# Two experts, one per token: dense passes for three of four batches replaced by blocks of 128 slots of one expert

## The chip, the cores and the metric

The kernel runs on one NeuronCore of a Trainium2 chip. The core has a matrix engine (TensorE, PE in the profile), a vector engine (VectorE, DVE), a scalar engine with function tables (ScalarE, ACT), a general engine (GpSimd, POOL) and SyncE (SP), which here only issues DMA transfers. The engines run beside each other and wait for each other by semaphores. The metric is the device time of one execution in microseconds (us); lower is better. The time before is the median of three runs, 1477.36 us (1475.82 to 1480.7).

## The reference, cut to what matters

`x` has 4 batches of 256 tokens of 256 numbers (`B`=4, `S`=256, `D`=256), all fp32. It goes through four layers, each a cross attention to 512 context rows and then a feed-forward part of a different kind, each on the layer norm of `x` and added to `x`. The change touches the feed-forward part of layer 2:

```python
scores = jax.nn.softmax(jnp.einsum('bsh,eh->bse', x, Wg), axis=-1)
top_expert = jnp.argmax(scores, axis=-1)
h0 = jax.nn.gelu(jnp.einsum('bsh,fh->bsf', x, W0a) + b0a, approximate=False)
out0 = jnp.einsum('bsf,hf->bsh', h0, W0b) + b0b
h1 = jax.nn.relu(jnp.einsum('bsh,fh->bsf', x, W1a) + b1a)
out1 = jnp.einsum('bsf,hf->bsh', h1, W1b) + b1b
mask0 = (top_expert == 0).astype(x.dtype)[..., None]
return out0 * mask0 + out1 * (1.0 - mask0)
```

Every token takes the output of one of two experts, and the experts differ in their weights and in their function (gelu or relu). Each has a hidden width of 512 (`F2`). The cross attention of layers 1 to 3 has 16 heads of 128 over 512 context rows. Layer 1's feed-forward part has eight experts, two for each token.

## The kernel before

The whole program is one long list of instructions for each engine, written out by hand: within `tc.manual_schedule` the order of TensorE, ScalarE, VectorE and GpSimd is the order of the calls in the code, and SyncE's DMAs also go in program order. A token's row lies on a partition, 128 tokens to a chunk, two chunks to a batch (`NC`=2). Where a matmul needs the features on partitions, TensorE transposes the chunk against the identity and ScalarE copies the result from PSUM.

**Attention 2** (`attention(2, ...)`) runs over 32 units, four batches by eight pairs of heads (`b`, `hp`). In each unit, TensorE makes the next unit's queries (`seven`, L1785, with VectorE putting the products together in `four`, L1794 to L1798), then four score matmuls and four context matmuls of 512 columns (`heads`, L1815 and L1821) with ScalarE's exponentials (L1818) between. GpSimd adds exponentials in halves (L1832, for the last unit L1830), VectorE sums them (`summed`, L1840 to L1846). For each quarter of a batch (four units), `quotients` takes the reciprocal of the sums (a matmul `pz`, L1853), `divided` spreads it (L1867) and multiplies the heads' outputs by it on GpSimd (L1868), `o_sums` makes sums of blocks on GpSimd (L1710 to L1713), and `Output` multiplies with the folded output weights (`pao`, `pbo`). The very last quarter goes through `last_output` (`py`, L1903), which is plain matmuls. A callback `after(b, hp)` is called at the end of each unit, so other work can be woven in: in attention 2 it is `beside2`. A second callback, `at_end`, is called before `last_output`.

`beside2` adds layer 1's last outputs (`Back`, whose indirect DMAs on GpSimd fetch rows), loads weights, and for the batches that are done computes the layer norm that layer 2's experts need: `Norm` (statistics on VectorE, a power on GpSimd L920) at hp 4, `tokens` (two VectorE operations, L925) at hp 5, `turned2` (four transposes L2484, a copy on ScalarE L2485) at hp 6. The last batch's is done after attention 2.

**Layer 2's experts** follow as a dense pass: for each batch `chosen2` computes the two logits with small matmuls of two columns (L2547) and a mask; `rise2` computes both experts' hidden layer for all 256 tokens (L2527, 16 matmuls of 256 columns; gelu with bias on ScalarE L2535, relu with bias on VectorE L2539); `fall2` computes both outputs (L2564, 16 matmuls of 256 columns for a batch), adds the bias (L2572) and adds output times mask to `x_sb` (L2574). In between stand the eight steps of `fold`, which multiply layer 3's attention weights together (`pm` L985, `pn` L1001, copies L993 and L1004) from raw weights that SyncE loads (`load_raw`). After it come `layernorm_T` of batch 0 for attention 3, and `bound` (L1666 to L1684), three small matmuls with VectorE maxima between, which check that the folded weights keep the exponentials in range.

**Layer 1's experts**, earlier in the program, use the scheme that the change brings to layer 2: tokens are ranked by expert, a list of tokens per block is made with matmuls, an indirect DMA gathers a block's rows (L2294), the expert's number is loaded into registers (`values_load`, L2308), and the block's weights are copied from the big weight tile by that register (L2313).

## Time and profile before

| what | value |
|---|---|
| median of three runs | 1477.36 us |
| the profiled execution | 1483.07 us |
| its span, first to last instruction | 1481.3 us |
| mean granted TensorE clock | 0.989 of full |
| attention 2, with scores | 713.5 to 1009.3 us |
| end of attention 2 | 1009.3 to 1043.4 us |
| layer 2's experts, with the folds | 1043.4 to 1119.8 us |
| attention 3 | 1119.8 to 1455 us |

How to read the profile: a row of a group has the line of the code, the engine, the operation, the tiles it writes and reads (the program's names, without numbers), how often it ran, and its durations. An fp32 matmul leaves two records. Matmuls are pipelined, so the length of one record is longer than the time between two. Rows of a timeline have start, duration, engine, line, operation and tiles, and in brackets how long the engine sat idle before it and what released it. Rows of a stage table have the stretch, its length, and then the busy time of TensorE, its weight loads, VectorE, ScalarE and GpSimd with the number of instructions, the granted clock, and what DMA did. "Chain" is the chain of work that ended last, followed back from the end.

### The profile page before, as it was taken

The numbers are of one execution on the slowest core, as the hardware profiler recorded it, in microseconds if no ns is written. First come the engines' busy times: TensorE is split into PE (matmuls) and PEld (weight loads), VectorE is DVE, ScalarE is ACT, GpSimd is POOL, SyncE is SP. The second block draws the span as 40 slices with busy tenths as digits, with TensorE's granted clock in tenths as the row PEclk, the third lists the DMA queues.
The fourth block names the chain that finished last, engine by engine and source line by source line (L and its number), as shares of the span: only waits on it lengthen the run. The fifth ranks groups of instructions, "written<-read, shape, count | busy, mean of one in ns | idle before, by whom it ended". The sixth has DMA issues, their size and how long they took to land.

```text
span 1481.3 us, 20094 instructions
## 1 busy us (share of the span) xinstructions
PE 1445.1 (98%) x7457; PEld 955.4 (64%) x7457; DVE 905.6 (61%) x1953; ACT 576.1 (39%) x1111; POOL 664.4 (45%) x780
## 2 busy tenths in 40 slices
PE   8999999999999999999999999999999999999997
PEld 7666567565566666877555666665886566666656
DVE  5566774566666556543666665656445666767675
ACT  4566443433433332244543333333233433333341
POOL 2122232476555454131466655656003665455560
PEclk8899999999999999999999999999999999999999
DMA  5000021210000000163110000000310100000000
GB/s 164 2 1 2 24 84 36 71 38 0 8 1 8 1 0 30 47 202 98 43 51 5 11 1 1 1 0 0 107 36 29 33 1 1 1 1 0 1 0 32
DMA packets 47270, 43.38 MB, mean 29 GB/s; under 512 B 8057, under 2 KB 43610, under 8 KB 47164
## 3 DMA queue, kind: packets, MB, share of 16 engines
q1 hardware_dynamic: 44188, 35.59, 7.9%
q0 software_dynamic: 1872, 5.11, 1.3%
q8 instruction: 61, 1.00, 0.3%
q10 hardware_dynamic: 1104, 1.31, 0.3%
q14 instruction: 45, 0.37, 0.1%
HBM read 36.89 MB, written 5.11 MB: 28 GB/s over the span
## 4 chain that ended last, share of the span: by engine, by line
PE 88%; DVE 6%; POOL 3%; issue 2%; ACT 0%; DVEq 0%; POOLq 0%
PE ps L1815 21%; PE po L1821 21%; PE paq L1785 5%; PE pao L1785 4%; PE pbq L1785 4%; PE pbo L1785 3%; PE pgu L2321 2%; PE ph L2527 2%; PE po L2564 2%; PE ps L1321 2%; PE po L1331 2%; PE pyf L1448 2%; PE paf L1398 1%; PE py L1903 1%; PE pm L985 1%
## 5 line engine op out<-in xcount | busy, mean ns | idle before, releaser
L1832 POOL TENSOR_TENSOR half<-pT 128x1024 f32<-128x1024 f32 x93 | 218.9, 2354 | 371.6 <-ACT pT L1818 327.9
L1815 PE MATMUL ps<-qT,cT 128*128 128x512 f32 x768 | 345.5, 592 | 0.0
L1821 PE MATMUL po<-pT,c_sb 128*128 128x512 f32 x768 | 345.2, 592 | 0.0
L1818 ACT ACTIVATE pT<-ps,mbias 128x512 f32<-128x512 f32 x384 | 263.9, 687 | 154.7 <-PE ps L1815 143.4
L1821 PEld LDWEIGHTS po<-pT,c_sb 128*128 128x128 f32 x768 | 145.9, 190 | 183.7 <-issue 183.7
L1815 PEld LDWEIGHTS ps<-qT,cT 128*128 128x128 f32 x768 | 138.8, 190 | 137.9 <-issue 137.2
L1825 ACT COPY oT<-po 128x512 f32<-128x512 f32 x96 | 56.3, 587 | 263.5 <-PE po L1821 263.5
L1868 POOL TENSOR_TENSOR oT<-oT,wide 128x512 f32<-128x512 f32 x90 | 116.3, 1312 | 28.8 <-DVE wide L1867 28.8
L1325 ACT ACTIVATE pT<-ps 128x512 f32<-128x512 f32 x128 | 66.1, 602 | 44.2 <-PE ps L1321 44.0
L1795 DVE TENSOR_TENSOR qT<-qT,paq 128x128 f32<-128x128 f32 x90 | 25.5, 283 | 87.5 <-ACT qT L1794 87.4
L1840 DVE TENSOR_TENSOR half<-half 128x512 f32<-128x512 f32 x96 | 72.2, 752 | 8.1 <-POOL half L1832 4.4
L1795 DVE TENSOR_TENSOR w<-w,pao 128x128 f32<-128x128 f32 x21 | 6.0, 286 | 109.2 <-ACT w L1794 109.2
L1842 DVE STREAM_TRANSPOSE turned<-half 128x512 f32<-128x512 f32 x96 | 68.3, 711 | 6.3
L1785 PEld LDWEIGHTS paq<-xnT_a,m_sb 128*128 128x128 f32 x360 | 58.0, 191 | 21.5 <-PE po L1821 10.5
L1785 PE MATMUL paq<-xnT_a,m_sb 128*128 128x128 f32 x360 | 71.1, 279 | 0.1
L1785 PE MATMUL paq<-xx,m_x 128*128 128x128 f32 x360 | 69.8, 276 | 0.0
L1846 DVE TENSOR_REDUCE sums<-turned 128x16 f32<-128x512 f32 x96 | 65.8, 686 | 3.3
L1785 PE MATMUL pao<-n_x,ox 128*128 128x128 f32 x336 | 65.2, 276 | 0.3 <-POOL ox L1711 0.3
L1867 DVE STREAM_TRANSPOSE wide<-rz 128x512 f32<-128x512 f32 x96 | 62.2, 685 | 0.1
L1794 ACT COPY qT<-paq 128x128 f32<-128x128 f32 x90 | 24.0, 266 | 87.1 <-PE paq L1785 87.1
L1798 DVE TENSOR_TENSOR qT<-qT,pbq 128x384 f32<-128x384 f32 x90 | 49.8, 554 | 9.4
L1785 PEld LDWEIGHTS paq<-xx,m_x 128*128 128x128 f32 x360 | 54.7, 192 | 0.1
(397 smaller groups left out, 2614.3 us busy)
## 6 DMA issues: line engine op xcount, KB each, us to landing
wo<-in_L_wo SPq DMA_DIRECT2D x12, 512.0 KB
wq<-in_L_wqT SPq DMA_DIRECT2D x11, 512.0 KB
yd<-yr SPq DMA_DIRECT2D x23, 128.0 KB
w<-in_F_w SPq DMA_DIRECT2D x4, 512.0 KB
wk<-in_L_wkT SPq DMA_DIRECT2D x11, 128.0 KB
wv<-in_L_wvT SPq DMA_DIRECT2D x11, 128.0 KB
x_sb<-in_x SPq DMA_DIRECT2D x4, 256.0 KB
wa<-in_F_aT SPq DMA_DIRECT2D x1, 1024.0 KB
```

What stands on the lines that cost most here:

```text
L1325: nc.scalar.activation(pT[kp][:, j], ps[j], AF.Exp)
L1785: nc.tensor.matmul(p[:, at, :], lhsT=lhsT, rhs=rhs, start=(k == 0 and at == 0), stop=(k == len(of) - 1 and i == which[-1]),)
L1815: nc.tensor.matmul(ps, lhsT=cT[:, b, k * P : (k + 1) * P], rhs=qT, start=True, stop=True)
L1818: nc.scalar.activation(pT[:, k, :], ps, AF.Exp, bias=mbias[:, b, k : k + 1])
L1821: nc.tensor.matmul(po, lhsT=c_sb[:, b, k, :], rhs=pT[:, k], start=(k == 0), stop=(k == NK - 1))
L1825: done["head"] = nc.scalar.copy(raw, po).ins
L1832: nc.gpsimd.tensor_tensor(half, pT[:, 0:2], pT[:, 2:4], ALU.add)
L1840: nc.vector.tensor_tensor(part, half[:, 0], half[:, 1], ALU.add)
L1842: nc.vector.transpose(turned.rearrange("p f i -> p (f i)"), part)
L1846: nc.vector.tensor_reduce(sums[b, hp // 4][:, hp % 4, :], turned, AX.X, ALU.add)
L1867: nc.vector.transpose(wide, rzs[b, hp // 4][:, hp % 4, :, None].to_broadcast([P, NB, 32]))
L1868: eng.tensor_tensor(outs[b, hp], outs[b, hp], wide.rearrange("p f i -> p (f i)"), ALU.mult)
```

## The change

For batches 0 to 2 (768 tokens in 6 chunks) each token is computed by its own expert only. The tokens are ranked within attention 2, those of expert 0 and those of expert 1 fill separate blocks, 7 blocks of 128 slots in all, and each block is one expert's. Batch 3, whose attention ends last, stays dense.

- In `beside2`, `Norm` and `tokens` come two units and one unit earlier. The normed rows are written to DRAM (`xd2`) by SyncE. The logits are now made by four VectorE operations per batch that multiply and sum along the row (`chosen2`), with the router's weights spread over all partitions. `turned2` is gone. In the last batch's units, `ranks2` (hp 5: three small matmuls, some two dozen VectorE operations) and `lists2` (hp 6: six small matmuls) make the lists; then blocks 0 and 1 are gathered by GpSimd's indirect DMAs and their first weights copied (hp 6), and blocks 2 and 3 gathered (hp 7).
- At the end of attention 2 and before `last_output`, `end2` transposes two blocks and computes the first block's hidden matmuls.
- In the block loop, block j+1's hidden layer is computed ahead of block j's output. The function is chosen with multipliers: ScalarE computes the gelu, GpSimd the relu times 0 or 1, VectorE puts them together (`either`). ScalarE copies the second weights by register, VectorE the first ones. The output rows go to DRAM (`yd2`), and `Back2` gathers them into the tokens' order on GpSimd, six times, and adds them to `x_sb`.
- Batch 3's dense pass follows the loop, with the eight folds after and between it instead of through the whole pass.
- `bound` is cut in pieces with `yield`, which are run in attention 3 at b=0, hp 3, 5 and 7.

```diff
--- before.py
+++ after.py
@@ -1669,10 +1669,12 @@
...
         nc.vector.tensor_reduce(bm[:1], pb[:1, :], AX.X, ALU.max)
+        yield
...
         nc.vector.tensor_reduce(bc[: B * NK], pc[: B * NK, :], AX.X, ALU.max)
+        yield
...
         nc.vector.tensor_scalar(over, bm[:1], -1.0, 1.0, ALU.mult, ALU.add)
+        yield
...
+    N6 = (B - 1) * NC
+    NBLK2 = (N6 * P + 2 * (P - 1)) // P
+    FK = F2 // P
+    FA = ND * F2 + FK
...
-    def turned2(b, xn):
...
+    def chosen2(xn, name):
+        lg = small.tile([P, NC, 2], F32, tag="lg2", name=f"lg2_{name}")
         for c in range(NC):
+            for e in range(2):
+                all_ = f2x.tile([P, D], F32, tag="all2", name=f"all2_{name}_{c}_{e}")
+                nc.vector.scalar_tensor_tensor(
+                    all_, xn[:, c, :], 1.0, wg2[:, :, e], ALU.mult, ALU.mult, accum_out=lg[:, c, e : e + 1]
+                )
+        return lg
+    def taken_by(b, xn):
+        lg = chosen2(xn, f"{b}")
...
+    def ranks2():
+        pr = bank("t", [P, N6 + 1], "prank2")
+        nc.tensor.matmul(pr[:, :N6], lhsT=utri, rhs=takes2, start=True, stop=False)
+        nc.tensor.matmul(pr[:, :N6], lhsT=ones, rhs=taken2[:, :N6], start=False, stop=True)
+        nc.tensor.matmul(pr[:, N6:], lhsT=ones, rhs=taken2[:, N6:], start=True, stop=True)
+        rk = tile2("rk", [P, N6 + 1])
+        nc.vector.tensor_copy(rk, pr)
...
+        nc.vector.tensor_tensor(slot, slot, d, ALU.add)
...
+        for n in range(N6):
+            nc.vector.tensor_scalar(ats[n // NC][:, n % NC, :], lane2, ln[:, n : n + 1], None, ALU.is_equal)
+        sel = tile2("sel", [P, 2, NBLK2])
+        nc.vector.tensor_scalar(sel[:, 1], begins2[:, :NBLK2], nb, None, ALU.is_ge)
+        nc.vector.tensor_scalar(sel[:, 0], sel[:, 1], -1.0, 1.0, ALU.mult, ALU.add)
+        ebi = tile2("ebi", [1, NBLK2], I32)
+        nc.vector.tensor_copy(ebi, sel[:1, 1])
+        where = tile2("where", [P, N6], I32)
+        nc.vector.tensor_copy(where, slot)
+        state2.update(bring=bring, ats=ats, sel=sel, ebi=ebi, where=where)
+    def lists2():
+        pl = bank("t", [P, NBLK2], "plist2")
+        for n in range(N6):
+            nc.tensor.matmul(
+                pl, lhsT=state2["ats"][n // NC][:, n % NC, :], rhs=state2["bring"][:, n, :],
+                start=(n == 0), stop=(n == N6 - 1),
+            )
+        who = state2["who"] = tile2("who", [P, NBLK2], I32)
+        nc.vector.tensor_copy(who, pl)
+    class Block2:
+        def __init__(self, j):
+            self.j = j
+        def gather(self):
+            self.xg = state2["pool"].tile([P, D], F32, tag="xg", name=f"xg2_{self.j}", bufs=4)
+            nc.gpsimd.indirect_dma_start(
+                out=self.xg, out_offset=None, in_=xd2[:, :],
+                in_offset=bass.IndirectOffsetOnAxis(ap=state2["who"][:, self.j : self.j + 1], axis=0),
+            )
+        def turn_in(self):
+            pt = bank("t", [P, ND, P], f"pxg2_{self.j}")
             for d in range(ND):
-                nc.tensor.transpose(pt[:, d, c * P : (c + 1) * P], xn[:, c, d * P : (d + 1) * P], ident)
-        nc.scalar.copy(xnT2[b], pt)
+                nc.tensor.transpose(pt[:, d, :], self.xg[:, d * P : (d + 1) * P], ident)
+            self.xgT = state2["pool"].tile([P, ND, P], F32, tag="xgT", name=f"xgT2_{self.j}", bufs=3)
+            nc.scalar.copy(self.xgT, pt)
+        def weights(self):
+            j = self.j
+            self.e = nc.values_load(
+                state2["ebi"][0:1, j : j + 1], engines=[E.DVE, E.Activation], min_val=0, max_val=1,
+                skip_runtime_bounds_check_because="the outcome of a comparison",
+            )
+            self.wa = f2x.tile([P, FA], F32, tag="wa", name=f"wa2_{j}", bufs=2)
+            nc.vector.tensor_copy(self.wa[:, None, :], w2a[:, bass.ds(self.e, 1), :])
+        def others(self, fp):
+            self.wb = fp.tile([P, FK, D], F32, tag="wb", name=f"wb2_{self.j}")
+            nc.scalar.copy(self.wb[:, None], w2b[:, bass.ds(self.e, 1)])
+        def rise(self):
+            j = self.j
+            ph = bank("s", [P, FK, P], f"pb2_{j}")
+            for k in range(FK):
+                for d in range(ND):
+                    nc.tensor.matmul(
+                        ph[:, k, :], lhsT=self.wa[:, d * F2 + k * P : d * F2 + (k + 1) * P], rhs=self.xgT[:, d, :],
+                        start=(k == 0 and d == 0), stop=(k == FK - 1 and d == ND - 1),
+                    )
+            self.z = f2x.tile([P, FK, P], F32, tag="z2", name=f"z2_{j}")
+            nc.vector.tensor_tensor(
+                self.z, ph, self.wa[:, ND * F2 :, None].to_broadcast([P, FK, P]), ALU.add
+            )
+        def gelu(self, fp):
+            j = self.j
+            self.g = fp.tile([P, FK, P], F32, tag="g2", name=f"g2_{j}")
+            nc.scalar.activation(self.g, self.z, AF.Gelu)
+            self.r = fp.tile([P, FK, P], F32, tag="r2", name=f"r2_{j}")
+            nc.gpsimd.tensor_scalar(self.r, self.z, 0.0, state2["sel"][:, 1, j : j + 1], ALU.max, ALU.mult)
+        def either(self, fp):
+            j = self.j
+            self.h = fp.tile([P, FK, P], F32, tag="hb2", name=f"hb2_{j}")
+            nc.vector.scalar_tensor_tensor(
+                self.h, self.g, state2["sel"][:, 0, j : j + 1], self.r, ALU.mult, ALU.add
+            )
+        def fall(self, fp):
+            j = self.j
+            py = bank("mm", [P, D], f"pyb2_{j}")
+            for k in range(FK):
+                nc.tensor.matmul(
+                    py, lhsT=self.h[:, k, :], rhs=self.wb[:, k, :], start=(k == 0), stop=(k == FK - 1)
+                )
+            y = fp.tile([P, D], F32, tag="yb2", name=f"yb2_{j}", bufs=3)
+            done["slots2"] = nc.vector.tensor_tensor(y[:, None, :], py[:, None, :], b2b[:, bass.ds(self.e, 1), :], ALU.add).ins
+            nc.sync.dma_start(yd2[j * P : (j + 1) * P, :], y)
+    class Back2:
+        def __init__(self, n):
+            self.b, self.c = divmod(n, NC)
+            self.y = state2["pool"].tile([P, D], F32, tag="xg", name=f"yg2_{n}", bufs=4)
+            nc.gpsimd.indirect_dma_start(
+                out=self.y, out_offset=None, in_=yd2[:, :],
+                in_offset=bass.IndirectOffsetOnAxis(ap=state2["where"][:, n : n + 1], axis=0),
+            )
+        def add(self):
+            xc = x_sb[self.b][:, self.c, :]
+            nc.vector.tensor_tensor(xc, xc, self.y, ALU.add)
+    blocks2 = [Block2(j) for j in range(NBLK2)]
 
     def beside2(b, hp):
@@ -2494,115 +2685,139 @@
             backs[rows_from[at]] = Back(rows_from[at])
         if at - 2 in rows_from:
             backs[rows_from[at - 2]].add()
+        if at == 16:
+            back.close()
+            state2["pool"] = f2r.enter_context(tc.tile_pool(name="f2r", bufs=1, side="right"))
         if b == 0:
             load_waiting(1 if hp < 4 else 5)
         if b > 0:
-            if hp == 4:
+            if hp == 3:
                 ahead2[b] = Norm(b - 1, f"f2_{b - 1}")
-            elif hp == 5:
-                ahead2[b] = ahead2[b].tokens()
+            elif hp == 4:
+                xn = ahead2[b].tokens()
+                nc.sync.dma_start(xd2[(b - 1) * S : b * S, :].rearrange("(c p) d -> p c d", p=P), xn)
+                taken_by(b - 1, xn)
+        if b == B - 1:
+            if hp == 5:
+                ranks2()
             elif hp == 6:
-                turned2(b - 1, ahead2[b])
+                lists2()
+                for j in range(2):
+                    blocks2[j].gather()
+                    blocks2[j].weights()
+            elif hp == 7:
+                for j in range(2, 4):
+                    blocks2[j].gather()
+
+    def end2():
+        nc.scalar.preload_act_table_set("gelu_and_others")
+        blocks2[0].turn_in()
+        blocks2[1].turn_in()
+        blocks2[0].rise()
     with tc.manual_schedule(engines={E.PE, E.Activation, E.DVE, E.Pool}):
-        attention(2, *mn, first_xnT=first_xnT, after=beside2)
-        back.close()
+        attention(2, *mn, first_xnT=first_xnT, after=beside2, at_end=end2)
         with tc.tile_pool(name="f2", bufs=2) as fp, tc.tile_pool(name="raw3", bufs=4) as rawp:
             for i in range(2):
                 load_raw(3, i)
...
             mn = folded(3)
             fold = folding(3, *mn)
-            norm = Norm(B - 1, f"f2_{B - 1}")
-            chosen2(0)
-            rise2(0, range(2))
-            xn = norm.tokens()
-            rise2(0, range(2, 4))
-            turned2(B - 1, xn)
-            for b in range(B):
-                if b + 1 < B:
-                    chosen2(b + 1)
-                    rise2(b + 1, range(2))
-                fall2(b, 0)
-                if b == 1:
+            backs = {}
+            blocks2[0].gelu(fp)
+            blocks2[0].others(fp)
+            blocks2[0].either(fp)
+            norm = Norm(lastb, f"f2_{lastb}")
+            for j in range(NBLK2):
+                if j + 2 < NBLK2:
+                    blocks2[j + 2].turn_in()
+                if j + 1 < NBLK2:
+                    blocks2[j + 1].rise()
+                    blocks2[j + 1].gelu(fp)
+                    blocks2[j + 1].others(fp)
+                if j + 2 < NBLK2:
+                    blocks2[j + 2].weights()
+                if j + 1 < NBLK2:
+                    blocks2[j + 1].either(fp)
+                if j == 0:
+                    xn = norm.tokens()
+                elif j == 1:
+                    xnT2 = layernorm_T(xn, f"f2_{lastb}")
+                elif j == 2:
+                    lg = chosen2(xn, "last")
+                    nc.vector.tensor_tensor(mk2[:, :, 0], lg[:, :, 0], lg[:, :, 1], ALU.is_ge)
+                    nc.vector.tensor_scalar(mk2[:, :, 1], mk2[:, :, 0], -1.0, 1.0, ALU.mult, ALU.add)
+                if j + 1 == NBLK2:
+                    rise2(range(2))
+                blocks2[j].fall(fp)
+                if j + 4 < NBLK2:
+                    blocks2[j + 4].gather()
+                if j in (2, 4):
+                    load_raw(3, j // 2 + 1, done["slots2"])
+            for n in range(2):
+                backs[n] = Back2(n)
+            rise2(range(2, FK))
+            nc.scalar.preload_act_table_set("exp_and_others")
+            next(fold)
+            fall2(0)
+            next(fold)
+            fall2(1)
+            for n in range(2, 8):
+                if n < 4:
+                    backs[n - 2].add()
+                elif n - 2 in backs:
+                    backs[n - 2].add()
+                if n < N6:
+                    backs[n] = Back2(n)
+                if n == 4:
                     norm = Norm(0, "a3_0")
-                if b + 1 < B:
-                    rise2(b + 1, range(2, 4))
-                if b + 2 == B:
-                    nc.scalar.preload_act_table_set("exp_and_others")
-                fall2(b, 1)
-                if b < 2:
-                    load_raw(3, b + 2, done["fall2"])
-                if b == 1:
                     xn = norm.tokens()
-                if b == 2:
+                if n == 6:
                     xnT3 = layernorm_T(xn, "a3_0")
                 next(fold)
-                next(fold)
             next(fold, None)
-        bound()
+    f2r.close()
     f2s.close()
@@ -2818,9 +3033,13 @@
     routers = {}
+    bounds = bound()
     def beside3(b, hp):
         if b == 0:
             load_waiting(1 if hp < 4 else 5)
+            if hp in (3, 5, 7):
+                next(bounds)
         if b > 0:
             if hp == 4:
                 routers[b - 1] = Router(b - 1)
```

## The prediction

> **What bounds the kernel now.** I read the page's first parts, then a table of busy time by stage, then the groups and timelines of the stages that the diff touches. Page, busy time, TensorE's row in 40 slices and the chain by engine:
>
> ```profile
> PE 1445.1 (98%) x7457; PEld 955.4 (64%) x7457; DVE 905.6 (61%) x1953; ACT 576.1 (39%) x1111; POOL 664.4 (45%) x780
> ...
> PE   8999999999999999999999999999999999999997
> ...
> PE 88%; DVE 6%; POOL 3%; issue 2%; ACT 0%; DVEq 0%; POOLq 0%
> ```
>
> TensorE is the bound everywhere; another engine counts only where it makes TensorE wait. Stretches in order: attention 2, its end (no scores left to compute), layer 2's experts with the folds of layer 3's weights, attention 3, the rest:
>
> ```profile
> 713.50:1009.30 295.80, 294.59 (x1268) 179.96 (x1268) 182.09 (x373) 113.52 (x195) 170.97 (x195) 1.00 0.04 13
> 1009.30:1043.40 34.10, 33.11 (x155) 22.45 (x153) 23.69 (x36) 8.28 (x14) 21.65 (x25) 1.00 0.00 1
> 1043.40:1119.80 76.40, 75.10 (x379) 63.02 (x378) 34.43 (x89) 23.26 (x60) 1.39 (x2) 1.00 0.22 70
> ```
>
> The experts' stretch is 98% TensorE with VectorE at 45%, so columns taken off TensorE there are time. The end of attention 2 is the delicate one: 33.11 of 34.10 us for TensorE, but also 23.69 VectorE and 21.65 POOL. The chain gives the unit prices of the dense experts (start, us, what):
>
> ```profile
> 1043.65 7.01 PE ph L2527 x32
> ...
> 1052.83 3.56 PE ph L2527 x16
> 1056.39 3.45 PE po L2564 x16
> ...
> 1066.75 0.89 PE pm L985 x8
> 1067.64 0.86 PE pn L1001 x2
> ```
>
> An fp32 matmul is two records, so 16 matmuls of 256 columns are 6.95 us: 0.43 each, one of 128 columns (the 32 records of the pao group in 3.57 us) 0.223. A fold step is 8+2 records, 1.9 us.
>
> POOL's timeline at the end of attention 2 shows no gap for 20 us; its last lines, and TensorE's first waits after it:
>
> ```profile
> 1020.71 2.95 POOL L1868 TENSOR_TENSOR oT<-oT,wide 128x512 f32<-128x512 f32 x2
> ...
> 1027.90 1.26 POOL L1830 TENSOR_TENSOR half<-pT 128x512 f32<-128x512 f32 x1
> ```
> ```profile
> 1031.51 0.41 PE L1853 MATMUL pz<-sums,quad 128*128 128x64 f32 x2 [0.21 <-DVE sums L1846]
> ...
> 1034.90 1.99 PE L1903 MATMUL py<-n_sb,oT 128*128 128x256 f32 x8 [0.26 <-POOL oT L1868]
> 1037.42 5.45 PE L1903 MATMUL py<-n_sb,oT 128*128 128x256 f32 x24 [0.52 <-POOL oT L1868]
> ```
>
> So whatever is put on POOL or VectorE there makes pz, and all that follows, late almost one for one.
>
> **The change, part by part.** The experts' stretch, from the end of the last py matmul (1042.87) to attention 3's first pq (1119.81), is now 76.94 us: four batches at 6.95+6.9, eight folds 15.2, about 4 of routing matmuls (L2547, 8 records in 0.79 to 1.05 four times), transposes, and the bound check's three matmuls (1.2).
>
> *TensorE's new list in that stretch.* Five pairs of transposes (four pxn_f take 0.45) 1.1; rise of blocks 1 to 6, 8 matmuls of 128 columns, 6 x 1.79 = 10.7; fall of blocks 0 to 6, 4 of 256 columns, 7 x 1.72 = 12.0; two batches' transposes 0.9; dense batch 3 13.9; folds 15.2; layer 3's router transposes 0.6. Sum 54.4, against 76.9.
>
> *Stalls in the block loop.* Per block TensorE has 0.22+1.79+1.72 = 3.73 us of work. Between the end of rise(j+1) and rise(j+2) it has only fall(j) and two transposes, 1.94 us; in that time VectorE must do z2 and copy the next block's weights `wa`, whose register it loads first. Rows: z2 reads PSUM as L1004's copy does (0.69 us for 512), `wa` 0.70 from 0.544 for 736 (L2313), the register load 0.30. That is 1.7 plus hops: just covered, while VectorE has nothing else. It has: batch 3's Norm (two L925 and statistics) ahead of rise(2), and chosen2's four accumulating multiplies (L2666, 0.42 to 0.66, plus 0.08 each) ahead of rise(5). I put 1 to 1.8 and 1.5 on these, with the start and end of the loop 3.8 in all. Hidden, with cover: the gelu (0.69, L1818) and the copy of `wb` on ScalarE (1.05 from L2304's 0.37 for 256), since ScalarE has 1.8 us of work per 3.73; the merge hb2 (0.75 from L2574's 0.48 for 256) and y (L2572, 0.42), on VectorE behind them. Without cover they'd be seen 0.7 to 1.05 a block.
>
> *POOL against VectorE.* POOL's relu `r2` starts with z2's end, so just ahead of the `wa` copy. No POOL tensor-by-scalar operation is in the trace; the nearest row is the 128x512 multiply L1868, 1.26 to 1.31 us (1.72 at most), so r2 is between half that and 1.7; I take 1.3. Whether `wa` waits for it: L925, a VectorE operation with one large SBUF input like the copy, shows it.
>
> ```profile
> L925 DVE TENSOR_SCALAR xn_f<-x_sb,mv_f,rstd_f x24: 402/1355/1974, 142.2 to 1048.0; 128x256 f32<-128x256 f32 x24
> ...
> L2313 DVE COPY we<-wr x23: 543/544/585, 625.4 to 682.9; 128x736 f32 x23
> L2294 POOL DMA_INDIRECT xg<-xd,who x23: 943/979/1200, 615.0 to 672.3; - x23
> ```
>
> Minimum 402 ns, median 1355: beside POOL it waits. If `wa` waits for r2 wholly, a block has z2 0.69 + r2 1.3 + `wa` 0.7 + hops = 2.8 against 1.94, 0.9 for each of five blocks, 4.5; if not at all, 0. I take 2.5, since Norm's stalls overlap some. The last two lines (layer 1's experts) show that gathers do not have this price: 23 of them among 23 copies, neither stretched.
>
> Here the Trainium skill, "SBUF — State Buffer", § Who interferes with whom, agrees on the lock between computing VectorE and GpSimd operations and goes further: while VectorE runs a two-port copy, GpSimd cannot write the descriptors of its DMAs. By that rule the two `wa` copies put beside the two gathers at the end of attention 2 would delay POOL by another 1.4 (estimated from two copies of 0.70); by layer 1's rows it is nothing, and the rows have it.
>
> *The stretch's price*: 54.4+3.8+2.5 = 60.7, against 76.9: −16.2.
>
> *The end of attention 2.* TensorE gets rise(0) and two pairs of transposes (2.2), three ranking and six list matmuls (L2547's small ones run at about 0.12 a record, with waits 2.2), loses batch 2's four transposes (−0.45), and rise(0) fills waits of the py groups (0.26+0.52, −0.8): +3.2. Then the waits: ranks2 is about 24 VectorE operations, 0.16 to 0.28 each (six of them the 128x128 comparison, 0.276), 5 to 7.5 us against 2.2 idle ones (1018.56 to 1020.78). It stands in VectorE's queue ahead of four() of the last unit's queries, of the sums and of `wide`, for which POOL's 1020.71 multiplies wait. Two gathers (0.95+0.30 each, 2.5) stand on POOL ahead of the last o_sums and of half (L1830), and so of pz. pz comes 4.1 to 6.5 later, of which the matmuls above already fill 1.8: +2.3 to 4.7, I take 3.1. Sum +6.3. Gathers 2 and 3 stand behind half, and POOL idles 4.4 us after it. For the gelu's table (1.28, L2535), ScalarE idles 13 us before it.
>
> *Elsewhere.* The four transposes of batches 0 and 1 leave attention 2 (−0.9); Norm moves two units up and its two xn DMAs go to SP, where the stretch's DMA share is 0.04: nothing. Routing's multiplies are 2.5 us of VectorE per batch in units of 9.2 us where it is 62% busy: nothing, for 0.5 or so if they delay a four(). The bound check's pieces cost their matmuls inside attention 3, +0.6; their 1.2 at the end is in the 76.9. Back2: six gathers on POOL, idle there, each landing 2 us later beside 1.9 us of fold and more; attention 3's first matmul needs batch 0 alone, whose two come first. SP: y's seven 128 KB writes ahead of two loads of raw weights, which the folds need 10 us later: nothing, or 1 to 2 if late.
>
> **Sum**: −16.2 +6.3 −0.3 = −10.2, call it −10. All durations are from the profiled execution, 1483.07 us, span 1481.3; that is 0.4% above the median 1477.36, and I take the difference off the median: 1467.
>
> **Rivals.** *All hidden.* Columns alone: 54.4−76.9+3.2−0.3 = −19.6; with the 2 to 4 us of waits that I see no way round, −16 to −19: 1458 to 1461. For it: layer 1's blocks run with 73.23 of 75 us busy on the same scheme. Against: POOL has no compute step there.
>
> *The tail eats it.* If the ranking's small operations cost 0.3 each rather than 0.2 (+2.4), the lists wait a unit longer (+2), every `wa` waits for r2 (+2) and Back2's last gather holds attention 3 (+2), the gain is 2: 1473 to 1478. For it: POOL without a gap and waits passed on one for one. Against: they would have to come together.
>
> *Slower: the relu on POOL.* Per block z2 0.69, then r2 = R, then `wa` 0.70 behind it, hb2 0.75, y 0.42, 0.2 of hops: 2.76+R on VectorE's cycle. At R=1.3 this is 4.06, about what I charged. Each further us of R is 7 us over the loop: the gain of 10 is gone at R=2.7, and 0.3% slower at R=3.4, with 1490 at 4.6. For it: no such operation in the trace, and POOL's 128x1024 sums take 2.35, so R=2.35 needs only half the speed per element. Against: the rows of the same tile size. The skill's "GPSIMD Engine Reference", § 3.1, would make r2 0.77 for one input of 512 (an estimate by its cycles), and `wa`'s wait 0.4 a block instead of 0.9: 1.5 us less in the sum.
>
> *It doesn't do what it says*: TensorE's columns in the two programs can be counted, 948,846 before and 938,885 after, at 0.857 us per 512 a difference of 16.7; excluded.
>
> **How the numbers follow.** Likeliest case 0.57: −5 to −15, from wa 0 to 4.5, the tail 4 to 9, stalls 2.5 to 6: 1462 to 1472. All hidden 0.16. Tail eats it 0.14, which spans the line of 0.3% (4.4 us, about what a measurement of this kernel can tell from no change: 1472.9 to 1481.8); I give it 0.11 of same and 0.03 of faster. Slower by POOL, 0.13. Faster 0.57+0.16+0.03 = 0.76. The range leaves out 0.05 below 1458 and 0.15 above 1477.
>
> **What would show it.** Right: the loop's period near 4.1 us, `wa` copies of 0.7 to 1.8 right behind r2 and TensorE waiting for them; pz about 5 us later against its po; the stretch from last py to first pq near 61 us. Wrong: r2 above 2.5 us; the loop at 3.8; waits for the ranks' results (plist2 waiting on VectorE for more than 1 us), for xg2_0 (rise(0) behind a gather), or for the last Back2 gather in front of attention 3, which I take to land 2 us early.

## The result, and the profile after

The changed kernel takes 1478.69 us in the median (1473.03 to 1482.05), the one before 1478.28 (1475.7 to 1487.18). The ratio is 0.9992, with a 95% interval of 0.9979 to 1.0006: no difference. The prediction was 1467, faster by 10 us, and its range ended at 1477. The profiled execution took 1479.09 us, its span 1477.3.

The page after, busy time and the chain by engine:

```profile
PE 1432.4 (97%) x7421; PEld 943.6 (64%) x7421; DVE 914.9 (62%) x2007; ACT 582.7 (39%) x1117; POOL 695.6 (47%) x803
...
PE 86%; DVE 7%; POOL 4%; issue 1%; ACT 1%; DMA 0%; DVEq 0%; POOLq 0%
```

TensorE lost 12.7 us of busy time, although this sum also holds the parts that ran at half clock; POOL gained 31. DMA has come into the chain. Now the stages, cut at the same events in both kernels: the start of attention 2, the end of its third-last unit, the end of the last py matmul, the start of attention 3 (stretch, its length, busy time of TensorE, weight loads, VectorE, ScalarE, GpSimd, then the granted clock). The kernel before:

```profile
713.40:1011.80 298.40, 297.19 (x1273) 181.15 (x1273) 184.59 (x375) 113.62 (x195) 173.35 (x197) 1.00 0.04 13
1011.80:1042.90 31.10, 30.11 (x144) 20.86 (x142) 20.69 (x32) 8.28 (x14) 19.27 (x24) 1.00 0.00 1
1042.90:1119.80 76.90, 75.60 (x383) 63.52 (x382) 34.93 (x90) 23.26 (x60) 1.39 (x2) 1.00 0.22 69
```

And after:

```profile
711.10:1008.60 297.50, 296.29 (x1265) 180.37 (x1265) 184.65 (x409) 112.73 (x193) 173.48 (x197) 1.00 0.06 16
1008.60:1051.70 43.10, 38.74 (x177) 28.17 (x176) 30.05 (x59) 9.82 (x16) 23.57 (x28) 0.88 0.05 13
1051.70:1115.50 63.80, 55.86 (x318) 45.69 (x317) 33.30 (x79) 28.61 (x66) 27.53 (x18) 1.00 0.39 116
```

The reader is to see three things. The experts' stretch is 13.1 us shorter, yet TensorE is busy there for only 88% of it. The end of attention 2 is 12.0 us longer, and TensorE is idle for 4.4 us of it. And the granted clock there is 0.88, where it was 1.00 before. That column is the one that the prediction did not use. (The changed kernel's attention 2 starts 2.3 us earlier in this execution; the code up to there is the same but for loads, and half clock at the start of the program fell in other places.)

TensorE's timeline at the end of attention 2, after (start, us, line, matmul, and in brackets the wait ahead of it):

```profile
1017.74 1.40 PE L2578 MATMUL plist<-bring,at 128*128 128x7 f32 x12
1019.86 5.40 PE L1818 MATMUL ps<-qT,cT 128*128 128x512 f32 x8 [0.72 <-DVE qT L1801]
1025.09 3.60 PE L1824 MATMUL po<-pT,c_sb 128*128 128x512 f32 x8
...
1036.04 0.69 PE L1856 MATMUL pz<-sums,quad 128*128 128x64 f32 x2 [2.71 <-DVE sums L1849]
1036.52 0.74 PE L1788 MATMUL pbo<-n_sb,oT 128*128 128x128 f32 x2
1037.06 0.63 PE L1788 MATMUL pbo<-n_sb,ox 128*128 128x128 f32 x2
```

The last scores take 5.40 us where the same eight records take 3.60 elsewhere; a pbo pair stands 0.43 from the next, where it was 0.22. Both come right behind a wait.

The granted clock takes two values in the traces, 1.00 and 0.5. The half clock comes in pieces of 3.41 us or a multiple of it, mostly 3.4 or 6.8 (one piece near the start of the kernel before is 13.7, and the last piece is cut off by the end). So each execution's time can be split: time times mean granted clock (called full-clock time here) and the rest (the clock's loss). The rest counts the half clock also where TensorE is idle anyway, so it is an upper bound. Means with standard errors (before: the executions beside which the experiments ran; in those four groups its full-clock mean is 1466.6 to 1466.75, so the changed kernel, which ran at another time, can be set beside the experiments):

| kernel | executions | mean us | full-clock time | clock's loss |
|---|---|---|---|---|
| before | 82 | 1478.8 ± 0.3 | 1466.7 ± 0.1 | 12.1 ± 0.3 |
| after | 22 | 1477.7 ± 0.6 | 1461.3 ± 0.2 | 16.3 ± 0.7 |

Nearly all of the spread of a kernel, 9 us in the changed one, is in the second part: its full-clock time has a standard deviation of 0.8 us. The change saves 5.3 us at full clock instead of 10, and pays 4.2 back through the clock. Two questions follow: which waits took half of the gain, and does the clock really follow them?

### The profile page after: what moved, and what is told of

Its sections match the earlier page's. It is cut to its first block, busy times and chain, and to the rows that moved or that the text cites. A ratio compares the mean times of both kernels' runs of the same rounds, so it can differ in the third digit from the quotient of the medians.

```text
span 1477.3 us, 20232 instructions
## 1 busy us (share of the span) xinstructions
PE 1432.4 (97%) x7421; PEld 943.6 (64%) x7421; DVE 914.9 (62%) x2007; ACT 582.7 (39%) x1117; POOL 695.6 (47%) x803
## 4 chain that ended last, share of the span: by engine, by line
PE 86%; DVE 7%; POOL 4%; issue 1%; ACT 1%; DMA 0%; DVEq 0%; POOLq 0%
PE ps L1818 21%; PE po L1824 21%; PE paq L1788 5%; PE pao L1788 4%; PE pbo L1788 4%; PE pbq L1788 4%; PE pgu L2324 2%; PE ps L1321 2%; PE po L1331 2%; PE pyf L1448 2%; PE paf L1398 1%; PE py L1906 1%; PE psh L2160 1%; PE pyr L2343 1%; PE pn L1001 1%
## 5 line engine op out<-in xcount | busy, mean ns | idle before, releaser
L1871 POOL TENSOR_TENSOR oT<-oT,wide 128x512 f32<-128x512 f32 x90 | 116.0, 1308 | 31.5 <-DVE wide L1870 31.5
L1788 PEld LDWEIGHTS paq<-xnT_a,m_sb 128*128 128x128 f32 x360 | 57.9, 191 | 21.5 <-issue 10.6
```

The costliest lines, as they stand in the source:

```text
L1788: nc.tensor.matmul(p[:, at, :], lhsT=lhsT, rhs=rhs, start=(k == 0 and at == 0), stop=(k == len(of) - 1 and i == which[-1]),)
L1871: eng.tensor_tensor(outs[b, hp], outs[b, hp], wide.rearrange("p f i -> p (f i)"), ALU.mult)
```

## The experiments

Each is the changed kernel with the edit shown, but for one that starts from the kernel before. What they gave, in the same split:

| kernel | n | mean us | full clock | clock's loss | ratio to before (95%) |
|---|---|---|---|---|---|
| filler_before_pz | 12 | 1476.3 ± 1.1 | 1461.3 | 15.0 ± 1.1 | 0.9979 (0.9961 to 0.9997) |
| filler_tail_and_loop | 12 | 1476.1 ± 1.4 | 1461.3 | 14.8 ± 1.4 | 0.9978 (0.9954 to 1.0001) |
| before_late_sums | 12 | 1481.6 ± 0.8 | 1468.3 | 13.2 ± 0.9 | 1.0014 (0.9996 to 1.0031) |
| gathers_after_half | 12 | 1472.4 ± 1.0 | 1458.7 | 13.8 ± 1.1 | 0.9950 (0.9934 to 0.9967) |
| lists_spread | 8 | 1471.2 ± 1.0 | 1459.0 | 12.1 ± 1.0 | 0.9942 (0.9918 to 0.9966) |
| relu_on_vector | 6 | 1471.7 ± 0.7 | 1458.2 | 13.5 ± 0.5 | 0.9944 (0.9927 to 0.9961) |
| gathers_early | 12 | 1481.0 ± 1.2 | 1460.2 | 20.7 ± 1.3 | 1.0007 (0.9988 to 1.0026) |
| raw_loads_later | 12 | 1476.7 ± 1.1 | 1460.1 | 16.6 ± 1.1 | 0.9983 (0.9962 to 1.0005) |
| relu_spread_later | 6 | 1465.1 ± 0.8 | 1452.4 | 12.7 ± 0.9 | 0.9898 (0.9871 to 0.9925) |
| all_with_lighter_tail | 6 | 1465.1 ± 1.0 | 1452.6 | 12.5 ± 0.8 | 0.9900 (0.9871 to 0.9929) |
| lighter_tail_vector_copies | 6 | 1466.9 ± 1.5 | 1453.0 | 13.9 ± 1.6 | 0.9929 (0.9907 to 0.9950) |
| lighter_tail_norm_later | 4 | 1464.0 ± 0.1 | 1453.4 | 10.6 ± 0.4 | 0.9906 (0.9889 to 0.9922) |

### Does the clock follow the waits? Work added into a wait

```diff
-            out.products(lambda: quotients(B - 1, 1))
+            def fill():
+                if L == 2:
+                    junk = bank("mm", [P, D], "pfill")
+                    for i in range(6):
+                        nc.tensor.matmul(junk, lhsT=ident, rhs=x_sb[0][:, 0, :], start=True, stop=True)
+                quotients(B - 1, 1)
+            out.products(fill)
```

> Six matmuls of 256 columns (2.6 us at full clock) into a bank that nothing reads are put in front of pz in attention 2, where TensorE waits 2.71 us for the sums. Nothing else is changed and no wait is taken away. Theory A (the clock is halved because TensorE was idle): pz starts when it did, the pbo records run at 2.9 us instead of 5.1, so about 2 us less in the runs where the clock had dipped there. Rival B (the dip comes from something else): 0. Rival D (TensorE's work is what counts): 2.6 us more.

```diff
# as above, and in the block loop:
+                if j in (0, 2, 4):
+                    junk = bank("mm", [P, D], f"pfill_{j}")
+                    for i in range(3):
+                        nc.tensor.matmul(junk, lhsT=ident, rhs=x_sb[0][:, 0, :], start=True, stop=True)
                 if j + 2 < NBLK2:
                     blocks2[j + 2].turn_in()
```

> The changed kernel with 15 matmuls more that nothing reads (256 columns, 6.4 us at full clock): six in front of pz, three each at the start of the loop's passes 0, 2 and 4, which is where TensorE waits for hb2 and for the rows of blocks 4 and 6. Theory A (TensorE's waits in the tail and in the loop are what lowers the clock, 16.3 us lost to it on average against 12.2 before): full-clock time within 1 us of 1461.3, the loss falls to 12 to 13.5, so 1474 to 1475 in the mean although more is computed. Rival B (the clock does not follow the waits): the loss stays at 16, 1478. Rival D (the waits are too short to hold the added matmuls): full-clock time 3 to 6 us more.

The extra 2.6 and 6.4 us of matmuls cost nothing at full clock (1461.3 in all three): the waits hold them, and rival D is out. The time went down by 1.4 and 1.6 us against the changed kernel, which has a standard error of 1.3 and 1.5: the sign of theory A, but the loss did not fall to 12 to 13.5, so on the averages alone it is not shown. The profiles show it. The profiled execution of the second filler has the half-clock pieces at the same places as the changed kernel's up to the tail (at 21, 34.5, 140.5, 574 and 611.5 us), so the two can be laid side by side. Two stretches of the tail, first of the changed kernel, then with the fillers (the clock is the third number from the right):

```profile
1020.90:1024.30 3.40, 3.40 (x6) 1.46 (x5) 3.37 (x6) 1.49 (x3) 1.66 (x2) 0.53 0.00 0
...
1034.60:1041.30 6.70, 5.26 (x24) 5.26 (x25) 5.78 (x9) 0.34 (x1) 3.35 (x4) 0.51 0.13 39
```

```profile
1020.90:1024.30 3.40, 3.40 (x6) 1.49 (x5) 3.37 (x6) 1.42 (x3) 1.58 (x2) 0.54 0.00 0
...
1034.60:1041.30 6.70, 6.12 (x47) 5.38 (x46) 5.96 (x9) 1.13 (x3) 3.60 (x4) 1.00 0.15 42
```

The half clock behind the list's small matmuls, where no filler was put, is still there; the one behind pz's wait, which the filler covers, is gone, and in the same 6.7 us 47 matmul records ran instead of 24. In this pair of executions, then, filling the wait took the half clock away.

### One wait added to the kernel before

```diff
-                nc.vector.transpose(turned.rearrange("p f i -> p (f i)"), part)
+                for _ in range(5 if (L, b, hp) == (2, B - 1, H // 2 - 1) else 1):
+                    nc.vector.transpose(turned.rearrange("p f i -> p (f i)"), part)
```

> The kernel before, with one thing more: in attention 2's last unit the transpose ahead of the last sums is done five times instead of once (the same result), 4 x 0.71 = 2.84 us of VectorE, so that pz waits about 3 us instead of 0.21. TensorE's work is the same. The time is read as two parts, the time times the mean granted clock (what it would be at full clock) and the rest (what the half clock took). Theory A (a wait of this size there lowers the clock): full-clock time 2.6 us more, and the half clock takes 1.5 to 3.4 us more, 4 to 6 us in all. Rival B (the clock is not tied to the wait): 2.6 to 2.8 us in all, the second part as before.

In the profiled execution, the slowest of the twelve, pz waits 3.20 us, and the pbo pairs behind it are 0.43 us apart:

```profile
1034.50 0.66 PE L1854 MATMUL pz<-sums,quad 128*128 128x64 f32 x2 [3.20 <-DVE sums L1847]
1034.95 0.74 PE L1785 MATMUL pbo<-n_sb,oT 128*128 128x128 f32 x2
1035.48 0.63 PE L1785 MATMUL pbo<-n_sb,ox 128*128 128x128 f32 x2
```

This is a second pair that can be laid side by side: up to there the half-clock pieces lie where they lie in the kernel before (at 19.8, 33.4 and 610.3 us in both), and the added wait has brought one more, 6.8 us from 1033.5, where the kernel before has none. On average the edit costs 2.7 ± 0.9 us, 1.6 of it at full clock and 1.1 ± 0.9 by the clock. Theory A's 4 to 6 was too much; the total is that of rival B, though the split is between the two. That lies below what a piece in every execution would take (1.7 for 3.4 us, 3.4 for 6.8), though 1.7 is within its error. That a wait is not always answered can be seen without any edit, since the end of attention 1 has the same wait in all these kernels. The kernel before, and the changed one, each in its profiled execution:

```profile
577.16 0.41 PE L1853 MATMUL pz<-sums,quad 128*128 128x64 f32 x2 [2.64 <-DVE sums L1846]
577.40 0.44 PE L1785 MATMUL pbo<-n_sb,oT 128*128 128x128 f32 x2
577.68 0.39 PE L1785 MATMUL pbo<-n_sb,ox 128*128 128x128 f32 x2
```

```profile
574.55 0.66 PE L1856 MATMUL pz<-sums,quad 128*128 128x64 f32 x2 [2.65 <-DVE sums L1849]
575.00 0.74 PE L1788 MATMUL pbo<-n_sb,oT 128*128 128x128 f32 x2
575.53 0.63 PE L1788 MATMUL pbo<-n_sb,ox 128*128 128x128 f32 x2
```

The same wait, and only one of the two pays for it. The Trainium skill, "TensorE: Matmul & The Clock Gate", section "What's actually happening", gives a frame for it: the gate looks at windows of 3.41 us that run free of the program, so it depends on where a wait falls in them. The traces agree with that: in each of the fourteen, every change of the clock lies on one grid of 3.41 us, and this grid begins at different places after the program's start, from 0.5 to 3.4 us. Its threshold, a whole idle window of 3.4 us, does not agree: here 2.6 to 2.7 us of idle, and even 0.72 us behind 1.4 us of 7-column matmuls, were followed by half clock.

The traces also show what decides. Give each window of the grid the share of it in which matmuls stream columns, an estimate from the rows at 0.857 us for an fp32 matmul of 512 columns. There are 589 windows at full clock from 560 to 590 and from 1000 to 1120 us in the fourteen traces. Of the 20 with the least share, 0.21 to 0.37, 19 are followed by a window of half clock; of the others, at 0.38 and more, none is. So a wait of 2.65 us is paid for when most of it falls into one window (0.33 in the changed kernel at the end of attention 1) and not when the grid cuts it in two (0.46 there in the kernel before). The 7-column matmuls stream next to nothing, which is why the list's window counts as 0.37. The estimate holds for the fp32 matmuls of these stages; other matmuls in the program do not follow it.

### The tail: who is late?

```diff
             elif hp == 6:
                 lists2()
                 for j in range(2):
-                    blocks2[j].gather()
                     blocks2[j].weights()
             elif hp == 7:
-                for j in range(2, 4):
+                for j in range(4):
                     blocks2[j].gather()
```

> The first two gathers are issued one unit later, so that all four stand on POOL behind the last half and none ahead of the last o_sums. Theory A (the gathers on POOL make pz late, and the wait then halves TensorE's granted clock): half starts 2.5 us earlier, pz's wait falls from 2.71 us to about 0.3, the wait of 0.46 on the last ox is gone, and the 24 pbo records take 2.9 us instead of 5.1: 5 to 6 us less. Rival B (only the wait counts, the clock's dip has another cause): about 3 us less, pbo still at 5.1. Rival C (the ranking's operations on VectorE are what is late, the gathers fit in beside): under 1 us less.

The mean is 5.3 us less than the changed kernel's, 2.7 at full clock and 2.6 ± 1.3 by the clock: theory A in size. Of its steps only the first is in the profile: counted from the multiplies on POOL ahead of it (L1871), half starts 2.1 us earlier (7.8 us behind them for 9.9). So pz came 2.1 us earlier against the start of the last scores (14.1 us behind them for 16.2), but these scores ran at full clock in this execution, so TensorE was there earlier as well, and the wait stayed, with half clock behind it:

```profile
1016.64 3.70 PE L1818 MATMUL ps<-qT,cT 128*128 128x512 f32 x8 [0.71 <-DVE qT L1801]
...
1030.73 0.43 PE L1856 MATMUL pz<-sums,quad 128*128 128x64 f32 x2 [2.70 <-DVE sums L1849]
```

So the gathers are part of the lateness. Another part stands on VectorE, for which POOL had been idle in the changed kernel ahead of those multiplies:

```profile
1022.64 2.95 POOL L1871 TENSOR_TENSOR oT<-oT,wide 128x512 f32<-128x512 f32 x2 [5.02 <-DVE wide L1870]
```

```diff
# the six `at` comparisons go into ats2(), which is called one unit later
             elif hp == 6:
-                lists2()
+                ats2()
                 for j in range(2):
-                    blocks2[j].gather()
                     blocks2[j].weights()
             elif hp == 7:
-                for j in range(2, 4):
+                lists2()
+                for j in range(4):
                     blocks2[j].gather()
```

> The ranking is spread: the six 128x128 comparisons and the first two weight copies at hp 6, the list matmuls and all four gathers at hp 7, behind the last head. Nothing of the ranking stands on VectorE ahead of the last queries, `wide` and so POOL's multiplies, and no gather ahead of the last half. Theory A (that is what makes pz and the last scores late): the waits of 0.72 in front of the last scores and of 2.7 in front of pz go, full-clock time 3 to 4 us less than the changed kernel's 1461.3, the half clock takes 3 to 4 us less: 6 to 8 us less in all. Rival B (the operations are late wherever they stand, for VectorE and POOL are full there): 2 us less.

6.5 us less than the changed kernel, the size of theory A, but from 2.3 at full clock, less than its 3 to 4, and 4.2 by the clock. The wait of 0.72 is gone. The one for pz was not (2.46), and the rest of the ranking, 5.4 us of small operations at hp 5, still stood on VectorE ahead of the last queries, the sums and `wide`:

```profile
1030.33 0.43 PE L1856 MATMUL pz<-sums,quad 128*128 128x64 f32 x2 [2.46 <-DVE sums L1849]
```

In the loop, the transposes of blocks 4 and 6 waited longer than in the changed kernel (2.18 and 1.79 us for 1.76 and 1.47), which takes some of the gain back.

### The block loop

The page's groups of the changed kernel for the relu, the weight copies and the gathers (min/median/max in ns):

```profile
L2641 POOL TENSOR_SCALAR r<-z,sel x7: 1997/2277/2296, 1051.9 to 1082.3; 128x512 f32<-128x512 f32 x7
...
L2613 DVE COPY wa<-w2a x7: 686/689/1755, 1023.1 to 1077.9; 128x1028 f32 x7
...
L2593 POOL DMA_INDIRECT xg<-xd,who x7: 945/1417/1595, 1025.8 to 1070.1; - x7
```

The relu takes 2.28 us, not 1.3. The copies keep their 0.69 in the loop: they start 0.3 us ahead of the relu, and it is the relu that stretches, from 2.00 without a copy beside it. At the end of attention 2, where POOL's multiply had started first, it was a copy that stretched, to 1.76. TensorE's waits in the loop (the longest):

```profile
1054.88 1.97 PE L2654 MATMUL pyb<-wb,hb 128*128 128x256 f32 x8 [1.22 <-DVE hb L2646]
...
1064.49 0.41 PE L2601 MATMUL pxg<-ident,xg 128*128 128x128 f32 x2 [1.76 <-DMA xg<-xd,who]
...
1074.25 0.41 PE L2601 MATMUL pxg<-ident,xg 128*128 128x128 f32 x2 [1.47 <-DMA xg<-xd,who]
...
1077.19 1.97 PE L2654 MATMUL pyb<-wb,hb 128*128 128x256 f32 x8 [0.69 <-DVE hb L2646]
...
1081.37 1.96 PE L2654 MATMUL pyb<-wb,hb 128*128 128x256 f32 x8 [0.43 <-DVE hb L2646]
```

All four waits for hb2, 2.7 us with one of 0.40, are the relu's: ahead of each VectorE is idle for r2. So is one of 1.01 for batch 3's normed rows, which stand behind hb2 on VectorE. The gathers', 3.2, stand behind the relu on POOL. From 1077.19 to 1081.37 a block without a gather takes 4.18 us.

```diff
-            nc.gpsimd.tensor_scalar(self.r, self.z, 0.0, state2["sel"][:, 1, j : j + 1], ALU.max, ALU.mult)
+            nc.vector.tensor_scalar(self.r, self.z, 0.0, state2["sel"][:, 1, j : j + 1], ALU.max, ALU.mult)
```

> The relu times 0 or 1 (r2) goes from POOL to VectorE, 128x512. Theory A (r2 at 2.0 to 2.3 us on POOL sets the loop's cycle of 4.18 us and holds back the gathers behind it): r2 costs 0.4 to 0.7 us on VectorE, the waits for hb2 (1.22, 0.40, 0.69, 0.43) go, the cycle falls to TensorE's 3.7, gathers go out 2 us earlier: 4 to 6 us less. Rival B (the gathers' latency sets the loop): only the waits for hb2 in blocks without a gather's wait go, 1 to 2 us less. Rival C (VectorE becomes the bound, since it has chosen2 and Norm as well): 0 or more time.

```profile
L2641 DVE TENSOR_SCALAR r<-z,sel x7: 481/486/488, 1047.6 to 1074.3; 128x512 f32<-128x512 f32 x7
```

0.49 us on VectorE instead of 2.28 on POOL. The mean falls by 6.0 us, the upper end of theory A, but only 3.1 of it at full clock; 2.8 ± 0.8 came by the clock, which the theory did not name. All waits for hb2 are gone; block 4's rows are still late (1.55), block 6's no longer. New ones for `wa` have come (0.83, 1.26 and 0.37), as VectorE has more to do: rival C in small. By the averages the loop too has waits that the clock answers. The changed kernel's own profile has no half clock in the loop, so this pair of profiles does not show it; in those of gathers_early and lighter_tail_norm_later a piece lies in the loop behind a wait (2.19 and 2.06 us).

```diff
         blocks2[1].turn_in()
+        for j in (4, 5):
+            blocks2[j].gather()
         blocks2[0].rise()
...
                     blocks2[j + 2].turn_in()
+                if j == 0:
+                    blocks2[6].gather()
...
-                if j + 4 < NBLK2:
-                    blocks2[j + 4].gather()
```

> The gathers of blocks 4 and 5 are issued before last_output, that of block 6 in the loop's first pass, where the buffers are free; the rest is as in the changed kernel. Theory A (TensorE's two waits of 1.76 and 1.47 us for gathered rows are a price of their own): 3.2 us less. Rival B (the cycle z2, r2, hb2, y of 4.18 us is right behind, and chosen2's 2.1 us on VectorE behind the second): the waits move to hb2, 1.4 us less or not even that.

The waits for rows are gone, but only 1.1 us at full clock were gained, as rival B said in size. The waits moved, though not to hb2: `wa` of block 5 is waited for 1.44 us, behind chosen2 on VectorE, and the normed rows 2.19 instead of 1.01. And the kernel became slower, since the clock's loss rose to 20.7. In its profile there is a piece of half clock right behind that longer wait: the gather of block 6 stands on POOL just ahead of block 1's relu, and what follows on VectorE (hb2, the normed rows) is late for TensorE:

```profile
1064.34 0.67 PE L937 MATMUL pxn_f<-ident,xn_f 128*128 128x128 f32 x4 [2.19 <-DVE xn_f L925]
...
1078.18 2.05 PE L2626 MATMUL pb<-xgT,wa 128*128 128x128 f32 x16 [1.44 <-DVE wa L2613]
```

Why this costs 4.4 us of clock on average, more than one piece of half clock, is not settled by one profile.

```diff
-            for i in range(2):
-                load_raw(3, i)
...
-                if j in (2, 4):
-                    load_raw(3, j // 2 + 1, done["slots2"])
+                if j in (1, 2, 3, 4):
+                    load_raw(3, j - 1, done["slots2"])
```

> The first two sets of raw weights for the folds (2.6 MB) are loaded behind blocks 1 and 2 instead of ahead of the loop, the others behind blocks 3 and 4. Theory A (they fill the DMA engines, share 0.79 from 1051 to 1060, while block 4's rows are fetched): the wait for these rows falls from 1.76 to under 1 us, 1 us less at full clock, block 6's wait may grow. Rival B (the gather is late because it is issued behind r2, 1.5 us on POOL and 2.6 to land): no difference.

1.2 us less at full clock, theory A. Block 4's rows are no longer late: its transposes wait 0.90 us for a copy on ScalarE, where they waited 1.76 for the rows. Block 6's rows are late by 0.97 instead of 1.47, and block 5's, which were in time, by 1.02. The mean moved by 0.9 ± 1.2, as the clock's loss did not change.

### Put together

```diff
# relu_on_vector, lists_spread, raw_loads_later, and:
-                elif j == 2:
+                elif j == NBLK2 - 1:
                     lg = chosen2(xn, "last")
```

> Four edits together: the relu on VectorE, the ranking spread as in lists_spread, the raw loads later, and batch 3's logits (four multiplies, 2.1 us of VectorE) in the last pass of the loop instead of the third. Theory A (waits of different places add up, and the clock follows them): full-clock time 1461.3 - 3.1 (relu) - 3.5 (spread) - 1 (loads) - 1 (logits) = about 1453, half-clock loss 10 to 12: 1463 to 1465. Rival B (the waits take each other's place): 1468 to 1471.

1452.4 at full clock, and 1465.1 in the mean: theory A, the waits of different places add up. The clock's loss is back near that of the kernel before, 12.7 for 12.1. This is 1% faster than the kernel before, with the same work on TensorE as the changed kernel. Three more kernels went after the waits that were left, two in the tail and one in the loop:

```diff
# the block numbers and masks go from ranks2() at hp 5 to blocks_of(), called at hp 6 ahead of ats2()
-            nc.vector.tensor_copy(self.wa[:, None, :], w2a[:, bass.ds(self.e, 1), :])
+            (nc.scalar.copy if j < 2 else nc.vector.tensor_copy)(self.wa[:, None, :], w2a[:, bass.ds(self.e, 1), :])
```

> relu_spread_later, with two edits more: the ranking's second half (block numbers, masks) goes from hp 5 to hp 6, and the first two weight copies from VectorE to ScalarE, which waits most of the time there. In relu_spread_later pz still waited 2.45 us: the ranking's 5 us on VectorE at hp 5 stand ahead of the last queries, the sums and `wide`, so POOL starts its multiplies late. Theory A (VectorE's queue at hp 5 is the cause): the wait for pz falls to under 1 us, full-clock time 1452.4 less 1.5 to 2.5, the clock's loss 12.7 less about 1: 1461 to 1463. Rival B (the second half is late at hp 6 too, in front of the sums): pz waits as long, 1465.

```profile
1022.60 3.70 PE L1824 MATMUL po<-pT,c_sb 128*128 128x512 f32 x8 [1.24 <-ACT pT L1821]
1031.05 0.33 PE L1856 MATMUL pz<-sums,quad 128*128 128x64 f32 x2
```

pz no longer waits, as theory A had it, but the last context matmuls wait for ScalarE, which had the copies in front of the exponentials. The gain at full clock is nil: the wait moved.

```diff
-            (nc.scalar.copy if j < 2 else nc.vector.tensor_copy)(self.wa[:, None, :], w2a[:, bass.ds(self.e, 1), :])
+            nc.vector.tensor_copy(self.wa[:, None, :], w2a[:, bass.ds(self.e, 1), :])
```

> all_with_lighter_tail with the first two weight copies back on VectorE, at hp 6 between the block numbers and the masks. There pz's wait was gone, but the last context matmuls waited 1.24 us for the exponentials, since ScalarE had the two copies and their register loads in front of them, so the time stayed. Theory A (the wait had only moved to ScalarE): the wait of 1.24 goes, pz waits under 1 us, full-clock time 1452.6 less about 1.2. Rival B (the copies then hold up the sums on VectorE): pz waits 1 to 2 us again, no gain.

The wait of 1.24 is gone, pz waits 1.01, the list 0.33: no gain (1453.0), rival B.

```diff
-            norm = Norm(lastb, f"f2_{lastb}")
             for j in range(NBLK2):
...
                 if j == 0:
-                    xn = norm.tokens()
+                    norm = Norm(lastb, f"f2_{lastb}")
                 elif j == 1:
+                    xn = norm.tokens()
+                elif j == 3:
                     xnT2 = layernorm_T(xn, f"f2_{lastb}")
```

> The same, and batch 3's layer norm one pass later in the block loop (statistics behind block 1's weights instead of ahead of the loop, normed rows a pass later, transposes two passes later). Theory A (the five statistics operations, 1.4 us of VectorE ahead of z2 of block 1, are the cause of rise(2)'s wait of 0.83 for its weights, and the transposes' copy on ScalarE of the wait of 0.76): 1 to 1.5 us less than lighter_tail_vector_copies. Rival B (VectorE's cycle is full, the wait comes back at a later block): no gain.

The wait of 0.83 is gone, the one of 0.76 came back at a later block, and block 4's rows are late by 2.06: no gain at full clock (1453.4), rival B. Its four executions have the smallest loss by the clock, 10.6. It and relu_spread_later cannot be told apart.

## Why the prediction was wrong, point by point

**The step that failed first: the sum was made as if the granted clock stayed the same.** The prediction counted the new waits at the end of attention 2 (3.1 us) at their own length. Measured between the same events in the two profiles, that part is longer by 12.0: matmuls 3.8, waits 3.4 (0.72 and 2.71 for 0.21, the two 0.46, less the 0.78 of py), and 4.5 because the last scores (5.2 us for 3.4) and pz with pbo (5.8 for 3.1) ran at half clock; 0.3 is left over. The prediction's own terms, 3.2 of matmuls and 3.1 of waits, were right together to a microsecond; the 4.5 was in none. Over all executions the clock's loss rose by 4.2.

**The sum by parts**, in the two profiled executions, foreseen and measured: attention 2 up to its last units −0.9 and −0.9; its end +6.3 and +12.0; the experts' stretch −16.2 and −13.1; attention 3 +0.6 and +1.2. So −10.2 was foreseen and −0.8 came. Of the 9.4 that are missing, 4.5 are the half clock, 1.2 the rest of attention 2's end, 3.1 the experts' stretch, 0.6 attention 3 with the bound check. (The two spans differ by 4.0: 2.3 lie ahead of attention 2 and 1.0 behind the last matmul.)

**pz's lateness.** Foreseen at 4.1 to 6.5 us, by the ranking's operations on VectorE and the gathers on POOL; half (L1833) started at 1032.53, 4.0 us behind po's end, where it stood 0.3 behind it before. Counted from the end of the third-last unit, pz came 7.7 later, 5.9 without the 1.8 of half clock in the scores. Right in size, and gathers_after_half and lists_spread show both causes. The way there was not clean: the ranking's 23 operations took 8.7 us on VectorE (0.38 each), not 5 to 7.5, and the terms given (2.8 to 5.3 and 2.5 us) add up to 5.3 to 7.8, for which the text took 4.1 to 6.5 without saying why.

**The experts' stretch** was put at 60.7 and is 63.9. TensorE is busy for 55.9 where its list said 54.4. The waits are 7.9 instead of 6.3. But they are others than those foreseen: 2.7 for hb2, 3.2 for gathered rows, 1.0 for the normed rows, 0.7 for a fold's copy on ScalarE, and 0.2 for `wa`. `wa` was to cost 5 to 6 us, by Norm, chosen2 and the lock with POOL. VectorE's copy goes first (0.3 us) and POOL pays (0.28). The page that the prediction weighed, "SBUF — State Buffer", § Who interferes with whom, says that whoever issues first gets the shared ports and the other waits, and the rows here agree; the prediction had assumed the other order from the L925 rows.

**r2 was mis-sized**: 1.3 taken, 1.7 the upper bound, 2.0 alone and 2.28 beside a copy measured. The estimate by the page "GPSIMD Engine Reference", 0.77, is further off still. The nearest row, a two-input multiply of the same tile, was no bound for a one-input operation with two scalars. The loop's cycle came out at 4.18 for the 4.06 foreseen, since `wa` ran beside r2 instead of behind it: two errors that cancelled in the number, not in the consequence. The rival "relu on POOL" had the cycle through the relu, with R short of its 2.7, though it too put `wa` in the cycle.

**The gathers** of blocks 4 to 6 are in no term of the sum. They are issued behind fall(j) and the next relu, and needed one pass later: 1.53 to 1.59 us on POOL for the 0.98 of layer 1, and TensorE goes on with the rows 3.6 (block 4) and 2.7 us (block 6) after that, with the DMA engines filled by raw weights. That makes 3.2 us of waits. raw_loads_later and relu_on_vector show both halves of the cause.

**What was right**: attention 2 up to its last units is 0.9 us shorter, as foreseen from the transposes; the added logits and the earlier Norm are hidden; Back2 does not hold attention 3. The bound check costs more than the 0.6 foreseen: attention 3 is 1.2 us longer, all of it in the three units that hold the check's pieces. The rival "the tail eats it" named 1473 to 1478, which holds the mean, but mostly by luck: of its four causes only the first came (the ranking's operations at 0.38 each); the lists did not wait a unit longer, `wa` did not wait for r2, and Back2 held nothing. The rival "all hidden" has a slip: −19.6 with 2 to 4 us of waits is −15.6 to −17.6.

## What to carry to other kernels

When TensorE is the bound, a wait of 1 to 3 us for it may cost more than its length: price it with a piece of half clock behind it (1.7 to 3.4 us where it strikes), ask how much matmul work is left around it in 3.4 us, and compare kernels by time times mean granted clock as well as by time, as that tells edits apart that the times alone hide. Work taken off TensorE is gained only where the engines that serve it have room: look at which engine's queue the replacement's small steps enter, and what stands behind them. A gather's lead is counted from where it stands in its queue, behind the compute steps ahead of it, to its first reader, not in loop indices.

## What the runs showed that was not expected

- Added matmuls made the changed kernel no slower: 6.4 us of them, in waits, cost 0 at full clock, and one of two half-clock pieces in the tail was gone.
- GpSimd's one-input relu of 128x512 fp32 with a scalar per partition took 2.0 us alone, its two-input multiply of the same size 1.27 in the median (1.26 to 1.73).
- The first gather behind a 128x512 step on POOL took 1.24 to 1.60 us in these tails and loops, behind the 128x2 power (L920) 1.02 to 1.18, and those that followed another gather mostly 0.94 to 0.96. The cause was not tried.
- An edit that took away the 3.2 us of waits for rows (gathers_early) made the kernel slower than the changed one by 3.3 ± 1.4 us in the mean, all of it by the clock.
- Whether a wait is answered with half clock could be read from the share of one 3.41 us window in which matmuls stream columns: 19 of the 20 windows at 0.37 or less were, none at 0.38 or more.
